# Layer 0 self attention of a two-layer block: norms of two groups' keys in three steps over three slots, and rounds of a choice spread over three slots

## The chip, the cores and the metric

The kernel runs on one core of one Trainium2 chip. The metric is device time in microseconds (us) of one execution, as the median of several. Five engines with instruction streams of their own matter: TensorE (PE; its weight loads are PEld), VectorE (DVE), ScalarE (ACT), GpSimd (POOL) and SyncE (SP), which here only issues DMAs. Each engine works its stream off in order, and waits on semaphores for the others.

## The reference, cut to what matters

The input is `x`, 64 sequences of 32 tokens of 256 features. Two layers follow, each a cross attention, a self attention and a feed-forward part, each added to `x`. The change lies in the stage of layer 0's self attention, during which the choice of blocks for layer 0's feed-forward part is made as well:

```python
x = x + _L0_attn_ref(_layernorm(x, axis=-1), g_norm, Wq, Wkv, Wout, g_out)
x = x + _L0_ffn_ref(_layernorm(x, axis=-1), Wr, br, W1, W2)

def _L0_attn_ref(x, g_norm, Wq, Wkv, Wout, g_out):   # 16 heads of 128, one k and v for all
    xn = _layernorm(x, g_norm)
    q = xn @ Wq
    k, v = split(xn @ Wkv)
    q = l2norm(q * 16) * 4
    k = l2norm(k) * 4
    attn = softmax(q k^T)                             # within one sequence of 32
    return _layernorm(merge_heads(attn @ v) @ Wout, g_out)

def _L0_ffn_ref(x, Wr, br, W1, W2):
    prob = softmax(x @ Wr.T + br)                     # 16 blocks of 64
    mask = ones at the 4 largest of prob, ties to the lower block
    h = gelu(x @ W1.T) * mask of the block
    return h @ W2.T
```

The self attention sees two layer norms in a row: the block's own, and the one inside with `g_norm`. Both need a reciprocal root of a variance plus 1e-5; the second variance follows from the first, as variance times the square of the first reciprocal root.

## The kernel before, in words

The 2048 tokens lie in 16 tiles `xs[0..15]` of 128 tokens by 256 features, in SBUF throughout; four tiles are a group (`g` 0 to 3). All arithmetic is float32.

The stage of layer 0's self attention ("stage B", tile pools `wB`, `psB`, `psBy`, `psB2`) has its order on TensorE, VectorE, ScalarE and GpSimd written out by hand: these four engines take their instructions in the order in which the Python code issues them (`tc.manual_schedule`). SP's order is made by a scheduler. The stage is a loop over slots `t` = 0 to 16. In the trace I let slot `t` begin with the first scores (`Sb`, L908) of tile `t`. A slot issues, in this order:

- `similar(t)`: scores `Sb` and sums of squares `ssb` (L916, from `q2b`, which GpSimd squared); then ScalarE's Sqrt of them (`rqb`, L925)
- `gather(t - 1)`: the weighted sums of the values for the tile before, `avb` (L955), with shares `pTb` that VectorE finished in the slot before (L945); VectorE and ScalarE copy them to `oTb`, two parts each (L960, L962)
- `scale(t)`: VectorE's reciprocal of `rqb` (L930, 3.34 us) and its product with the scores (L932)
- `square(t + 1)` on GpSimd (L896, four parts), then `power(t)`: ScalarE's Exp (L936)
- place 5, where extra steps are put
- `project(t - 1)`: 32 matmuls `yb` (L968), about 7.1 us; `norm_stats(t - 1)`: statistics of `yb` on VectorE and a Sqrt on ScalarE (`lns_bo`, L980)
- `share(t)`: sums of the exponentials (`denb`, L942), VectorE's reciprocal of them (L944, 3.35 us) and the product into `pTb` (L945)
- `norm_out(t - 1)`: VectorE makes `ynb` (L992); GpSimd multiplies it by the gain and adds it to `xs` (L993, L994)
- `rotate(t)`: nine products on GpSimd (L822 to L839) of some 10 us in all, for layer 1; `fetch(t + 1)`: DMA loads for the next; `write_pad(t)`: a DMA

Between them are the places 0 to 4. `query_part` at the places 0 to 3 makes the queries of later tiles (`qb`, L877; copied by ScalarE, L885), some ten parts ahead. Further steps go to a slot and a place with `at(slot, place, step)`; steps of one slot and place run in the order of their `at` calls. Two PSUM buffers with the tag `mm` are shared in turn by `qb`, `kvp`, `kTp`, the transposes `tp` and `tpr`, `hp`, `lpc` and `mTp`: a matmul into one waits until the buffer's last content was copied out.

The steps that bear on the change:

- `keys_norm(g)`, at (3, 5) for g = 2 and at (6, 5) for g = 3: statistics of four tiles on VectorE (`stats`, L174 and L175), both norms one after the other (`ln_group` with `twice=True`: `rstd_of` is an addition on VectorE, L163, a Sqrt on ScalarE, L165, and a reciprocal on VectorE, L167; two products, L183 and L184, between them), then ScalarE writes the four normed tiles (`ln_out`, L196). `keys_turn(g)` transposes them a slot or two later, at (4g - 4, 2), and `keys_of` makes keys and values (`kvp`, L364), `turn_keys` turns the keys.
- `choose_norm(g)`, at (4g + 5, 5): the norm for the choice, statistics and one Sqrt (`lnv_r`, `lns_r`, `lnr_r`, `lnh_r`), then four outputs of ScalarE (`xn_r`, L196). `choose_turn(g)`, at (4g + 6, 1): transposes (`tpr`, L642) and ScalarE's copies (`xTr`, L645).
- `choose_blocks(g)`, at (4g + 7, 5): matmuls `lpc`, a softmax of 16 values.
- `choose_best(g, work, rounds)`: each of four rounds (0 to 3) finds the largest value left and adds its block to the mask. A round is two reductions (L679, L684), three or more products and comparisons of 128 x 64 with two inputs (L681, L682, L688), for rounds 0 to 2 a SCALAR_TENSOR_TENSOR that takes the block out (L690), and for rounds 1 to 3 an addition to the mask (L692). For groups 0 and 1, rounds 0 and 1 are at (4g + 7, 5) and 2 and 3 at (4g + 8, 5). Group 2 has its first two at (15, 3).
- `choose_store(g)`, at (4g + 9, 2): four transposes of the mask (`mTp`, L699), VectorE's copy (L701), a DMA to `maskd` in DRAM (L702). `spread` reads it back, one row for 64 partitions, as `mb` (L708).
- From slot 13 on the feed-forward part of group 0 is worked in: `hp` (L716), ScalarE's Gelu (L723), VectorE's product with `mb` (L724).

Phase A, before this stage, has the other form of the reciprocal root, with `power=True`: an addition and a power of -0.5 on GpSimd (L159, L160).

Of the kernel before, what the change touches and what calls it, by code (L numbers as in the profile page):

```python
# [7 lines left out]
F32 = mybir.dt.float32  # L8
AF = mybir.ActivationFunctionType
ALU = mybir.AluOpType  # L10
# [3 lines left out]
P = 128  # L14
B, S, D = 64, 32, 256
NT = B * S // P
NG = NT // 4
# [10 lines left out]
EPS = 1e-5  # L28
# [11 lines left out]
def bc(ap, axis, n):  # L40

    shape = list(ap.shape)
    shape.insert(axis, n)
    return ap.unsqueeze(axis).to_broadcast(shape)
# [3 lines left out]
def perceiver_kernel(ctx: ExitStack, tc: tile.TileContext, a: dict, out: bass.AP):  # L48
    nc = tc.nc
# [21 lines left out]
    def sm(name, shape):  # L71
        return small.tile(shape, F32, tag=name.split("_")[0], name=name)
# [4 lines left out]
    xs = [x[:, :D] for x in xf]  # L77
# [69 lines left out]
    mhalf = const.tile([P, 4], F32, name="mhalf")  # L147
# [22 lines left out]
    def stats(mv_slot, src, name, sign=None):  # L170
        st = sm(f"lnb_{name}", [P, 6])
        if sign is not None:
            nc.vector.tensor_copy(st[:, 0:1], sign)
        nc.vector.bn_stats(st, src)  # L174
        nc.vector.bn_aggr(mv_slot, st)  # L175
# [16 lines left out]
    def ln_out(x_, rs, sh, i, name, act=False):  # L192

        y = xnp.tile([P, D], F32, tag="xn", name=f"xn_{name}_{i}")
        if act:
            nc.scalar.activation(  # L196
                y, x_, AF.Identity, scale=rs[:, i : i + 1], bias=sh[:, i : i + 1]
            )
        else:
            nc.vector.scalar_tensor_tensor(  # L200
                y,
                x_,
                rs[:, i : i + 1],
                sh[:, i : i + 1].to_broadcast([P, D]),
                ALU.mult,
                ALU.add,
            )
        return y

    def ln_group(g, name, twice=False, act=False, power=False, sign=None):  # L210

        mv = sm(f"lnm_{name}{g}", [P, 4, 2])
        for i in range(4):
            stats(mv[:, i, :], xs[4 * g + i], f"{name}{g}_{i}", sign)
        rs, sh = ln_scale(mv, f"{name}{g}", twice, power)
        return [ln_out(xs[4 * g + i], rs, sh, i, f"{name}{g}", act) for i in range(4)]
# [127 lines left out]
    latT = {}  # L344
# [4 lines left out]
    def keys_norm(g):  # L349
        latT[g] = ln_group(g, "b", twice=True, act=True, power=g == 0)  # L350

    def keys_turn(g, ps):
        latT[g] = transposed(latT[g], ps, g, "b", gain=gn)

    def keys_of(g, ps, part):

        xT = latT[g]
        if part == 0:
            keys[g] = kvp.tile([P, 4, D], F32, tag="kv", name=f"kvb{g}"), sm(f"ssk_b{g}", [P, 4])
        kv, ssk = keys[g]  # L360
        for i in range(2 * part, 2 * part + 2):
            kv_ps = ps.tile([P, D], F32, tag="mm", name=f"kvp{g}_{i}")
            for k in range(KC):
                nc.tensor.matmul(  # L364
                    kv_ps,
                    xT[:, k, i * P : (i + 1) * P],
                    b_kv[:, k, :],
                    start=(k == 0),
                    stop=(k == KC - 1),
                )  # L370
            nc.scalar.copy(kv[:, i, :], kv_ps)
            junk = kvp.tile([P, P], F32, tag="junk", name=f"junkb{g}_{i}")
            nc.scalar.activation(junk, kv[:, i, :P], AF.Square, accum_out=ssk[:, i : i + 1])
        if part == 1:
            sk = sm(f"sk_b{g}", [P, 4])
            nc.scalar.activation(sk, ssk, AF.Sqrt, bias=keps, scale=1.0 / 16.0)
            rk = sm(f"rk_b{g}", [P, 4])
            nc.vector.reciprocal(rk, sk)
            for i in range(4):
                nc.vector.tensor_scalar_mul(kv[:, i, :P], kv[:, i, :P], rk[:, i : i + 1])  # L380
            keys[g] = kv

    def turn_keys(g, ps):
        kv = keys[g]
        kT_ps = ps.tile([P, 512], F32, tag="mm", name=f"kTp{g}")
        for i in range(4):
            nc.tensor.transpose(kT_ps[:, i * P : (i + 1) * P], kv[:, i, :P], ident)
        kT = kvp.tile([P, 512], F32, tag="kT", name=f"kTb{g}")
        nc.vector.tensor_copy(kT, kT_ps)
        keys[g] = kT, kv  # L390
# [4 lines left out]
    with tc.tile_pool(name="wA", bufs=2) as work, tc.tile_pool(  # L395
        name="psA", bufs=1, space=PSUM
    ) as ps1, tc.tile_pool(
        name="psA2", bufs=2, space=PSUM
# [234 lines left out]
    def choose_norm(g, act=True):  # L633
        choice[g] = ln_group(g, "r", act=act)

    def choose_turn(g, ps, work):
        xn = choice[g]
        xT = choice[g] = work.tile([P, KC, 512], F32, tag="xTr", name=f"xTr{g}", bufs=1)
        for k in range(KC):
            tp = ps.tile([P, 512], F32, tag="mm", name=f"tpr{g}_{k}")  # L640
            for i in range(4):
                nc.tensor.transpose(  # L642
                    tp[:, i * P : (i + 1) * P], xn[i][:, k * P : (k + 1) * P], ident
                )
            nc.scalar.copy(xT[:, k, :], tp)  # L645
        return xT
# [28 lines left out]
    def choose_best(g, work, rounds):  # L675

        lg, mx, mask = choice[g]
        for r in rounds:
            nc.vector.tensor_reduce(mx, lg, AX.X, ALU.max)  # L679
            eq = work.tile([P, 4, 16], F32, tag="eq", name=f"eqc{g}_{r}", bufs=1)  # L680
            nc.vector.tensor_tensor(eq, lg, bc(mx, 2, 16), ALU.is_equal)  # L681
            nc.vector.tensor_tensor(eq, eq, bc(desc, 1, 4), ALU.mult)  # L682
            m2 = sm(f"m2c_{g}_{r}", [P, 4])
            nc.vector.tensor_reduce(m2, eq, AX.X, ALU.max)  # L684
            one = mask
            if r:
                one = work.tile([P, 4, 16], F32, tag="one", name=f"onec{g}_{r}", bufs=1)
            nc.vector.tensor_tensor(one, eq, bc(m2, 2, 16), ALU.is_equal)  # L688
            if r < 3:
                nc.vector.scalar_tensor_tensor(lg, one, -2.0, lg, ALU.mult, ALU.add)  # L690
            if r:
                nc.vector.tensor_add(mask, mask, one)  # L692

    def choose_store(g, ps, work):

        mask = choice.pop(g)[2]
        mT_ps = ps.tile([16, 512], F32, tag="mm", name=f"mTp{g}")
        for i in range(4):
            nc.tensor.transpose(mT_ps[:, i * P : (i + 1) * P], mask[:, i, :], ident)  # L699
        mT = const.tile([16, 512], F32, tag="mT", name=f"mTc{g}", bufs=1)  # L700
        nc.vector.tensor_copy(mT, mT_ps)  # L701
        nc.sync.dma_start(maskd[g], mT)  # L702
# [142 lines left out]
    with tc.tile_pool(name="wB", bufs=2) as work, tc.tile_pool(  # L845
        name="psB", bufs=1, space=PSUM
    ) as ps1, tc.tile_pool(name="psBy", bufs=1, space=PSUM) as ps_y, tc.tile_pool(
        name="psB2", bufs=2, space=PSUM
# [164 lines left out]

        steps = {}

        def at(slot, place, fn):
            steps.setdefault((slot, place), []).append(fn)

        for g in range(1, NG):
            at(4 * g - 4, 2, lambda g=g: keys_turn(g, ps2))
            slot, place_ = (0, 5) if g == 1 else (4 * g - 3, 1)
            at(slot, place_, lambda g=g: keys_of(g, ps2, 0))
            at(4 * g - 3, 3, lambda g=g: keys_of(g, ps2, 1))
            at(4 * g - 2, 2, lambda g=g: turn_keys(g, ps2))
            if g > 1:
                at((3, 6)[g - 2], 5, lambda g=g: keys_norm(g))
        for g in range(NG - 1):
            at(4 * g + 5, 5, lambda g=g: choose_norm(g))  # L1030
            at(4 * g + 6, 1, lambda g=g: choose_turn(g, ps2, work))
            at(4 * g + 7, 5, lambda g=g: choose_blocks(g, ps2, work))
            if g < NG - 2:
                at(4 * g + 7, 5, lambda g=g: choose_best(g, work, (0, 1)))
            at(4 * g + 8, 5, lambda g=g: choose_best(g, work, (2, 3)))
            if g < NG - 2:
                at(4 * g + 9, 2, lambda g=g: choose_store(g, ps2, work))
        ff, late = {}, []

        def ff_late():  # L1040
# [96 lines left out]
    with tc.tile_pool(name="wC", bufs=2) as work, tc.tile_pool(  # L1137
        name="psCh", bufs=2, space=PSUM
# [95 lines left out]
        latT = {}  # L1234
# [98 lines left out]
    with wd1:  # L1333
# [6 lines left out]
        with tc.tile_pool(name="wD", bufs=2) as work, tc.tile_pool(  # L1340
            name="psD", bufs=1, space=PSUM
        ) as ps1, tc.tile_pool(
            name="psD2", bufs=2, space=PSUM
# [288 lines left out]
            for pair in range(NB // 2):  # L1632


                b = 2 * pair
# [330 lines left out]
    with tc.tile_pool(name="wE", bufs=2) as work, tc.tile_pool(  # L1966
        name="psE", bufs=1, space=PSUM
# [7 lines left out]
        ps2 = ps1  # L1975
# [572 lines left out]
```

## Time and profile before

| what | value |
|---|---|
| three runs | 1151.64, 1155.46, 1159.72 us; median 1155.46 |
| profiled execution, its own time | 1160.48 us |
| its span, first to last instruction | 1158.6 us |
| mean granted TensorE clock | 0.984 |
| stage B in that span | about 145 to 486 us |

What the engines did in some slots (start of the slot to the next, in us; the shares of idle time follow by subtraction):

| slot | from, to | TensorE busy | VectorE busy | ScalarE busy | GpSimd busy |
|---|---|---|---|---|---|
| 1 | 159.33, 179.13 | 19.80 | 12.13 | 10.15 | 2.56 |
| 2 | 179.13, 197.56 | 18.43 | 10.91 | 7.99 | 14.87 |
| 3 | 197.56, 216.30 | 18.23 | 17.96 | 7.51 | 15.45 |
| 4 | 216.30, 237.86 | 19.16 | 14.10 | 10.81 | 14.68 |
| 6 | 259.89, 279.75 | 19.62 | 16.06 | 11.07 | 15.44 |
| 7 | 279.75, 299.53 | 19.78 | 17.74 | 7.81 | 15.42 |
| 8 | 299.53, 320.61 | 19.16 | 19.99 | 8.58 | 13.98 |
| 9 | 320.61, 343.31 | 22.25 | 19.54 | 12.79 | 16.89 |
| 11 | 363.18, 382.96 | 19.78 | 17.22 | 7.45 | 15.44 |
| 12 | 382.96, 403.61 | 19.15 | 19.84 | 8.48 | 14.32 |
| 13 | 403.61, 422.84 | 18.89 | 17.55 | 11.14 | 15.06 |
| 14 | 422.84, 443.60 | 19.26 | 15.85 | 13.60 | 18.21 |

How to read the lines of the profile: a line of the page's first part is an engine, its busy time, its share of the span and its number of instructions. A line of the table of waits is who waited for what: us in total, how often, the longest. A line of the timeline is start, duration, engine, line of the kernel, operation, output `<-` inputs, shapes and count; merged neighbours have one line, and in square brackets stands the idle time of the engine just before it and what ended that.

### The profile page before, as it was taken

Reading aid. Unit: us, or ns where it says so; the run is one execution under the profiler, and the core shown is the slowest. Engines: PE = TensorE matmul, PEld = TensorE weight load, DVE = VectorE, ACT = ScalarE, POOL = GpSimd, SP = SyncE. Lnnn points to the kernel's source line nnn. Section 1 sums busy time; section 2 is a strip of 40 time slices with the busy share of each in tenths; the row PEclk is TensorE's granted clock in tenths of the full one; section 3 lists DMA queues with packets and bytes.
Section 4 is the critical chain, followed back from the end, with each engine's and each line's share of the span. In section 5 each row is a group of like instructions: output and inputs, shape, how many; then the busy total and the mean of one; then the engine's idle time right before and its main releaser. Section 6 shows DMA issues by size and latency. Waiting matters only on the chain. (4 is left out here: it accounts for less than half of the span.)

```text
span 1158.6 us, 26394 instructions
## 1 busy us (share of the span) xinstructions
PE 1106.6 (96%) x10026; PEld 790.2 (68%) x10026; DVE 769.7 (66%) x1812; ACT 575.4 (50%) x1442; POOL 457.0 (39%) x766
## 2 busy tenths in 40 slices
PE   9999999899999999999998999999999989889997
PEld 5667766677767657667676777777777657555653
DVE  5786246868987987765215787777878565765532
ACT  2346363545355365231227777777777456542221
POOL 1444255777768787410001121121222356732111
PEclk9999999999999999999999999999999998989999
DMA  5131132546346446492213121223230044212413
GB/s 133 57 95 40 33 88 85 171 123 168 97 129 206 116 116 191 144 278 69 74 39 66 29 56 29 74 56 83 56 83 19 4 133 126 86 35 74 153 38 118
DMA packets 98990, 109.05 MB, mean 94 GB/s; under 512 B 37240, under 2 KB 73465, under 8 KB 98642
## 3 DMA queue, kind: packets, MB, share of 16 engines
q1 hardware_dynamic: 97138, 103.05, 31.5%
q0 software_dynamic: 1728, 4.33, 1.1%
q8 instruction: 80, 1.31, 0.5%
q14 instruction: 44, 0.36, 0.1%
HBM read 76.36 MB, written 31.41 MB: 93 GB/s over the span
## 5 line engine op out<-in xcount | busy, mean ns | idle before, releaser
L1469 ACT ACTIVATE pp<-Sd,nm 128x256 f32<-128x256 f32 x256 | 119.9, 482 | 40.4 <-POOL nm L1466 40.4
L877 PE MATMUL qb<-xT_b,b_q 128*128 128x256 f32 x512 | 122.2, 386 | 0.8 <-ACT qTb L885 0.8
L877 PEld LDWEIGHTS qb<-xT_b,b_q 128*128 128x128 f32 x512 | 94.9, 191 | 40.1 <-issue 19.3
L1465 DVE TENSOR_REDUCE nm<-Sd 128x2 f32<-128x512 f32 x128 | 79.5, 684 | 54.1 <-PE Sd L1452 54.1
L968 PE MATMUL yb<-b_o,oTb 128*128 128x256 f32 x512 | 114.9, 383 | 0.5 <-DVE oTb L960 0.5
L1466 POOL TENSOR_SCALAR nm<-nm 128x2 f32<-128x2 f32 x128 | 27.0, 211 | 221.6 <-DVE nm L1465 221.3
L968 PEld LDWEIGHTS yb<-b_o,oTb 128*128 128x128 f32 x512 | 97.2, 192 | 14.7 <-issue 1.6
L1487 DVE TENSOR_TENSOR pp<-pp,rd 128x512 f32<-128x512 f32 x128 | 89.6, 700 | 4.4
L1497 PE MATMUL pt<-cst,pp 128*128 128x128 f32 x512 | 68.3, 275 | 6.2 <-DVE pp L1487 5.2
L1503 ACT COPY pTd<-pt 128x512 f32<-128x512 f32 x128 | 68.8, 591 | 10.4 <-PE pt L1497 4.8
L896 POOL TENSOR_TENSOR q2b<-qTb 128x512 f32<-128x512 f32 x64 | 64.7, 1041 | 13.9 <-ACT qTb L885 13.9
L1497 PEld LDWEIGHTS pt<-cst,pp 128*128 128x128 f32 x512 | 59.4, 141 | 15.7 <-ACT ld L1477 5.0
L885 ACT COPY qTb<-qb 128x512 f32<-128x512 f32 x64 | 37.3, 584 | 63.9 <-PE qb L877 61.1
L930 DVE RECIPROCAL rqb<-rqb 128x512 f32<-128x512 f32 x16 | 53.5, 3344 | 17.1 <-ACT rqb L925 17.1
L1245 PE MATMUL qd<-xT_d,d_m 128*128 128x256 f32 x256 | 63.8, 393 | 0.7 <-DVE rd L1486 0.3
L1544 PE MATMUL yd<-d_n,co 128*128 128x256 f32 x256 | 63.2, 391 | 0.0
L1478 POOL TENSOR_TENSOR sd<-sd,ld 128x2 f32<-128x2 f32 x128 | 27.4, 214 | 86.0 <-ACT ld L1477 86.0
L1452 PE MATMUL Sd<-ct,qTd 64*128 64x256 f32 x480 | 60.0, 388 | 0.0
L731 PE MATMUL yc<-c,hc 128*128 128x256 f32 x256 | 58.5, 382 | 0.0
L1518 PE MATMUL od<-pTd,na 128*64 128x256 f32 x480 | 58.4, 385 | 0.0
L1544 PEld LDWEIGHTS yd<-d_n,co 128*128 128x128 f32 x256 | 46.2, 189 | 16.7 <-DVE nm L1465 7.7
L944 DVE RECIPROCAL rdb<-denb 128x512 f32<-128x512 f32 x16 | 53.7, 3354 | 5.8 <-PE denb L942 5.6
(429 smaller groups left out, 2416.8 us busy)
## 6 DMA issues: line engine op xcount, KB each, us to landing
srt<-pad SPq DMA_DIRECT2D x17, 1040.0 KB
mb<-maskd SPq DMA_DIRECT2D x64, 128.0 KB
ct<-ctd SPq DMA_DIRECT2D x30, 257.0 KB
rct<-in_ctxT_dram SPq DMA_DIRECT2D x32, 128.5 KB
rrt<-in_ctxT_dram SPq DMA_DIRECT2D x64, 64.2 KB
ctd<-rct SPq DMA_DIRECT2D x32, 128.5 KB
nad<-rna SPq DMA_DIRECT2D x16, 256.0 KB
fg<-in_f_wg_dram SPq DMA_DIRECT2D x16, 256.0 KB
```

Of the source, the lines that this page charges most:

```text
L731: nc.tensor.matmul(y_ps, hs[f][:, i * P : (i + 1) * P], c_2[:, f, :], start=(f == 0), stop=(f == 7),)
L877: nc.tensor.matmul(q_ps[:, hh, :], b_q[:, k, h * P : (h + 1) * P], xT[:, k, c0 : c0 + 256], start=(k == 0), stop=(k == KC - 1),)
L896: nc.gpsimd.tensor_tensor(q2[:, 4 * h4 : 4 * h4 + 4, :], q, q, ALU.mult)
L968: nc.tensor.matmul(y_ps, oT[:, h, :], b_o[:, h, :], start=(h == 0), stop=(h == NH - 1))
L1245: nc.tensor.matmul(q_ps[:, r, :], m[:, k, pr * P : (pr + 1) * P], xT[:, k, c0 : c0 + 256], start=(k == 0), stop=(k == KC - 1),)
L1452: nc.tensor.matmul(logits[b][hh][:, u, :], qT[hs, b % 8, 4 * u : 4 * u + 4, :], ct[hs, b % 4, :KEYS], start=True, stop=True,)
L1465: nc.vector.tensor_reduce(nm, s_ps[hh], AX.X, ALU.max, negate=True)
L1469: nc.scalar.activation(pb[:, u, hh, :], s_ps[hh][:, u, :], AF.Exp, bias=nm[:, u : u + 1], accum_out=sd[:, u : u + 1],)
L1487: nc.vector.tensor_tensor(pp, pp, bc(rd, 2, KEYS), ALU.mult)
L1497: nc.tensor.transpose(pts[c][:, hh * 256 + u * P : hh * 256 + u * P + P], probs[b][:, u, hh, c * P : (c + 1) * P], ident,)
L1503: nc.scalar.copy(pT[:, c, :], pt)
L1544: nc.tensor.matmul(y_ps, co[:, pr, :], n[:, pr, :], start=(pr == pr0), stop=(pr == pr0 + n_pr - 1),)
```

## The change

`keys_norm` of groups 2 and 3 is no longer one step of one slot. A new function `keys_norm_step(g, z)` has three: z = 0 takes the statistics and gives the first reciprocal root to GpSimd (an addition and a power); z = 1, a slot later, makes the second variance on VectorE and gives its reciprocal root to GpSimd; z = 2, another slot later, makes scale and shift on VectorE and has ScalarE write the tiles. The last step is in the slot and place in which all of it was before: slots 1, 2, 3 for group 2 and 4, 5, 6 for group 3. The small tiles between the steps are new ones of their own, four float32 values per partition each (eight for the statistics).

For groups 0 and 1 the four rounds are spread differently: round 0 stays in slot 4g + 7, rounds 1 and 2 are in slot 4g + 8, round 3 in slot 4g + 9, and `choose_store` is in slot 4g + 10 instead of 4g + 9, at place 2 as before. At (9, 5) and (13, 5) round 3 is issued ahead of `choose_norm` of the next group. Group 2 stays as it was.

```diff
+        begun = {}
+
+        def keys_norm_step(g, z):
+            if z == 0:
+                mv = work.tile([P, 4, 2], F32, name=f"kbm_{g}", bufs=1)
+                for i in range(4):
+                    stats(mv[:, i, :], xs[4 * g + i], f"b{g}_{i}")
+                r1 = work.tile([P, 4], F32, name=f"kbr_{g}", bufs=1)
+                nc.gpsimd.tensor_scalar(r1, mv[:, :, 1], EPS, None, ALU.add)
+                nc.gpsimd.tensor_tensor(r1, r1, mhalf[:, 0:4], ALU.pow)
+                begun[g] = mv, r1
+            elif z == 1:
+                mv, r1 = begun[g]
+                r2 = work.tile([P, 4], F32, name=f"kbq_{g}", bufs=1)
+                nc.vector.tensor_tensor(r2, mv[:, :, 1], r1, ALU.mult)
+                nc.vector.tensor_tensor(r2, r2, r1, ALU.mult)
+                nc.gpsimd.tensor_scalar(r2, r2, EPS, None, ALU.add)
+                nc.gpsimd.tensor_tensor(r2, r2, mhalf[:, 0:4], ALU.pow)
+                begun[g] = mv, r1, r2
+            else:
+                mv, r1, r2 = begun.pop(g)
+                nc.vector.tensor_tensor(r2, r2, r1, ALU.mult)
+                nc.vector.scalar_tensor_tensor(r1, mv[:, :, 0], -1.0, r2, ALU.mult, ALU.mult)
+                latT[g] = [ln_out(xs[4 * g + i], r2, r1, i, f"b{g}", True) for i in range(4)]
...
             if g > 1:
-                at((3, 6)[g - 2], 5, lambda g=g: keys_norm(g))
+                for z in range(3):
+                    at((1, 4)[g - 2] + z, 5, lambda g=g, z=z: keys_norm_step(g, z))
         for g in range(NG - 1):
             at(4 * g + 5, 5, lambda g=g: choose_norm(g))
             at(4 * g + 6, 1, lambda g=g: choose_turn(g, ps2, work))
             at(4 * g + 7, 5, lambda g=g: choose_blocks(g, ps2, work))
-            if g < NG - 2:
-                at(4 * g + 7, 5, lambda g=g: choose_best(g, work, (0, 1)))
-            at(4 * g + 8, 5, lambda g=g: choose_best(g, work, (2, 3)))
-            if g < NG - 2:
-                at(4 * g + 9, 2, lambda g=g: choose_store(g, ps2, work))
+            if g == NG - 2:
+                at(4 * g + 8, 5, lambda g=g: choose_best(g, work, (2, 3)))
+                continue
+            for z, rounds in enumerate(((0,), (1, 2), (3,))):
+                at(4 * g + 7 + z, 5, lambda g=g, rounds=rounds: choose_best(g, work, rounds))
+            at(4 * g + 10, 2, lambda g=g: choose_store(g, ps2, work))
```

## The prediction

> **What bounds the kernel now.** I read the busy shares first, then the waits of TensorE between 140 and 560 us, where the change lies, then each engine's timeline there, slot by slot.
>
> ```profile
> PE 1106.6 (96%) x10026; PEld 790.2 (68%) x10026; DVE 769.7 (66%) x1812; ACT 575.4 (50%) x1442; POOL 457.0 (39%) x766
> ```
>
> TensorE is the bound, so only idle time of TensorE can be won. Of the 420 us in that stretch, its waits for other engines add up to 11.5 us in the table of waits, and one row is nearly half of that (times, then the longest):
>
> ```profile
> PE avb L955 <- DVE pTb L945: 5.1, 3, 2.2
> ```
>
> The timeline shows the three places, the first matmuls of the weighted sums (`gather`) at the heads of slots 4, 8 and 12:
>
> ```profile
> 222.31 1.14 PE L955 MATMUL avb<-pTb,kvb 32*128 32x512 f32 x8 [2.16 <-DVE pTb L945]
> ...
> 305.06 1.14 PE L955 MATMUL avb<-pTb,kvb 32*128 32x512 f32 x8 [1.68 <-DVE pTb L945]
> ...
> 325.05 1.14 PE L955 MATMUL avb<-pTb,kvb 32*128 32x512 f32 x8
> ...
> 388.07 1.14 PE L955 MATMUL avb<-pTb,kvb 32*128 32x512 f32 x8 [1.26 <-DVE pTb L945]
> ```
>
> They are the slots after 3, 7 and 11: in 3 VectorE does `keys_norm(2)`, in 7 and 11 it does `choose_blocks` and two rounds. What else VectorE did there:
>
> ```profile
> 210.40 0.42 DVE L174 BATCH_NORM_STATS2 lnb_b<-x 128x6 f32<-128x256 f32 x1
> ...
> 212.65 1.03 DVE L163 TENSOR_SCALAR lnv_b<-lnm_b 128x4 f32<-128x4 f32 x1
> 213.96 0.18 DVE L167 RECIPROCAL lnr_b<-lns_b 128x4 f32<-128x4 f32 x1 [0.27 <-ACT lns_b L165]
> ...
> 217.44 0.43 DVE L174 BATCH_NORM_STATS2 lnb_bo<-yb 128x6 f32<-128x256 f32 x1
> ...
> 314.04 1.31 DVE L690 SCALAR_TENSOR_TENSOR lgc<-onec,lgc 128x64 f32<-128x64 f32 x1
> ...
> 324.27 0.69 DVE L945 TENSOR_TENSOR pTb<-pTb,rdb 128x512 f32<-128x512 f32 x1
> ```
>
> The norm of the keys occupies VectorE from 210.40 to 217.44, while the projection's result waited for it since 213.78 (the 7.14 us block of `yb` from 206.64). Slot 8 is the warning: VectorE ends its share at 324.96 and the sums start at 325.05 without a wait. It is as tight as a slot can be, and so is slot 12 (407.62 against 407.70).
>
> **Part 1: norms of the keys in three steps.** Slot 3 keeps two small operations (0.16 us each alone, up to 1 us beside GpSimd) of 7.04 us. The share then ends some 3.6 us earlier, bounded by the projection's end, and the 2.16 us go. GpSimd starts its next rotation as much earlier, so the squares for slot 5 are no longer late (from the scores at 237.86 to the sums of squares it is 1.28 us, elsewhere 0.88: 0.4 won). The moved pieces: four pairs of statistics, 2.1 us, go into slots 1 and 4, where VectorE sits idle 5.3 and 6.6 us for the projection; two products (0.16 to 0.96 us each) into slots 2 and 5, idle 5.1 and 2.4. These idle times are the cover; without it the 2.1 us would be late time of the share. The Sqrt of ScalarE becomes an addition and a power on GpSimd, 0.23 and 1.04 us by the rows of `lnr_b`. They queue ahead of `norm_out`'s two products, for which GpSimd idles anyway (14.3, 2.8, 2.1 and 5.9 us in slots 1, 2, 4, 5), and VectorE reads them a slot later. Slot 6 loses 6 us of VectorE but its sums had no wait. No table load goes: `lns_bo` needs the Sqrt table right after. Sum: -2.56 us (-2.0 to -2.6).
>
> **Part 2: rounds 0 | 1, 2 | 3.** Slots 7 and 11 lose round 1 (297.40 to 300.18, 2.78 us; 2.79 in slot 11), which covers the waits of 1.68 and 1.26. But slots 8 and 12 now hold rounds 1 and 2 for 2 and 3: one SCALAR_TENSOR_TENSOR more. It took between 0.22 and 1.31 us in this trace; I take 0.96, as the last operation of that place did (319.20). Slot 8: VectorE starts 1.15 us after the sums of the slot, then 18.56 us as before, plus 0.96: 20.67. TensorE alone needs 19.99 less the 0.64 by which late squares held it: 19.35. So 1.3 us of the wait come back: net 1.68 + 0.64 - 1.35 = 0.97 won (0.6 to 1.7). Slot 12 in the same way: 0.35 won (0 to 1.1).
>
> **Part 3: round 3 ahead of `choose_norm`, in slots 9 and 13.** A round of six operations took 1.5 us with GpSimd idle (467.25 to 468.79) and 4.7 or 4.8 beside its rotation. In slot 9 it starts at the phase at which round 2 started in slot 8; its first five operations took 2.45 us there, with the last 3.3. The store's copy and its wait (1.32) leave, so `choose_norm(1)` comes 2.0 us later (0 to 3.4). VectorE has room (1.46 us idle and 3.1 us ahead of the sums). Who waits is ScalarE, in order behind this norm's Sqrt and four outputs:
>
> ```profile
> 341.61 0.59 ACT L885 COPY qTb<-qb 128x512 f32<-128x512 f32 x1 [1.51 <-PE qb L877]
> ```
>
> This copy has 1.51 us of room; it slips to about 341.9, while TensorE, 0.6 us earlier without the transposes of the mask, asks for that PSUM buffer in `keys_of`: 0.6 us lost (0 to 2.0). Slot 13 is worse, since ScalarE is full there:
>
> ```profile
> 419.25 0.20 ACT L165 ACTIVATE lns_r<-lnv_r 128x4 f32<-128x4 f32 x1 [0.61 <-DVE lnv_r L163]
> 420.59 2.08 ACT L196 ACTIVATE xn_r<-x,lnh_r,lnr_r 128x256 f32<-128x256 f32 x4 [1.13 <-DVE lnh_r L189]
> 422.57 0.19 ACT L980 ACTIVATE lns_bo<-lnv_bo 128x1 f32<-128x1 f32 x1
> ...
> 424.07 0.60 ACT L723 ACTIVATE hc<-hp 128x512 f32<-128x512 f32 x1
> ...
> 427.98 0.60 ACT L723 ACTIVATE hc<-hp 128x512 f32<-128x512 f32 x1
> ...
> 429.83 1.09 ACT L645 COPY xTr<-tpr 128x512 f32<-128x512 f32 x2
> ```
>
> From 420.59 to 430.92 it idles only 0.29 us (ahead of its copy of the sums at 428.87), and `hp` at 430.48 waits 0.71 us for one of these copies. What delays `lnv_r` reaches TensorE whole. The masked product now ends at 415.7 instead of 416.7 (no copy of the mask, an earlier Gelu); a round beside GpSimd, 4.0 us taken between 1.5 and 4.8, makes the statistics 3.1 us late (0.5 to 3.9). Less the 0.29, `hp` slips 2.8 us.
>
> **Part 4: the store a slot later.** Four transposes (0.44 us net) and a copy of 0.68 us go from slots 9 and 13 to 10 and 14; VectorE idles 2.5 and 2.9 us there. In 10 the transposes follow two users of the two PSUM buffers and wait some 0.3 us for a copy. In 14 they stand between two `hp`, so the second waits for the first one's Gelu: 0.85 us with the transposes (0.4 to 1.0). On SP's queue the store moves from 345 to about 367, and ten of the mask's 16 reads (6.2 us to issue) with it, ahead of the rotation's write, which goes out at 372.8 as soon as GpSimd is done, and of the next fetch. Held up by at most 6 us, that fetch still lands some 15 us before its use after 408, and the masks, read at 415, are there by 380: taken at nothing. Without that room each late microsecond would be GpSimd's or the product's. The second store moves alike, for masks read after 486.
>
> Sum: -2.56 - 0.97 - 0.35 + 0.6 + 0.3 + 2.8 + 0.85 = **+0.7 us**. The profiled execution took 1160.48 us at a span of 1158.6, so 1161.2 against itself; it stands 5.0 above the median of 1155.46, from which the forecast is **1156.2 us**. After 560 us nothing is touched and the whole shifts.
>
> The round's price deserves a second look. In the trace the two-input operation at L682 took between 0.217 and 1.314 us, so even the worst did not wait much longer than one GpSimd operation of 1.28. The Trainium skill's page "SBUF — State Buffer" (section "SBUF: two separate sides") says that GpSimd and a VectorE operation with two SBUF inputs take the shared port pair by an exclusive lock and that the loser blocks for the whole instruction. An estimate by that rule: each of a round's four two-input operations could wait 1.28 us, 6.4 us in all, and the total would be +6 us. No round in this trace reached that; 4.8 us is the most.
>
> **Rivals.** *Rounds are cheap in their new places* (25%): one operation more costs 0.22, and round 3 costs 1.5 us. Then part 2 wins 1.7 and 1.1, slot 9 loses none, slots 13 and 14 lose 0.3 + 0.85: -2.56 - 1.7 - 1.1 + 0.3 + 1.15 = -3.9, 1151.6 us. For it: the round at 467. Against it: GpSimd rotates from 327 and from 410 on, through both places. *Slower by ScalarE's queue in slot 13* (20%): round 3 at 4.8 us and a contended `lnv_r` (1.0 for 0.34 us) make the Gelus and copies of slot 13 another 1.5 us late, and the copy of slot 9 costs 2.0 for 0.6: +3.6, 1159.1 us. It decides from 3.3 us for that round on, where the sum passes zero. For it: two-input operations of 1.0 to 1.3 us all through the rotation; against it: the 2.45 us of the five operations from 311.59. *GpSimd becomes late by the powers* (5%): four times 1.27 us ahead of a rotation, passed on to the squares, make +5.1 on top of the sum, 1161.3 us; for it the three late squares in the waits (1.5 us), against it the idle times above. The forecast has the remaining 50%. That the edits change nothing in the order can be excluded, since these engines run in written order.
>
> **Numbers.** The cases span -3.9 to +5.8; the three runs before spread 4 us to either side of their median, so a median of three may be 1.5 off. Eight in ten: 1150.5 to 1162. One per cent is 11.6 us, about what can be told from no change, and no case reaches it: within 95%, faster 2%, slower 3%, for what the trace of before cannot show, such as other addresses in SBUF.
>
> **What would show it.** Right: no wait of `avb` at the heads of slots 4, 8 and 12, a wait of about 1 us at 9 and at 13; `hp` of slot 14 waiting some 3 us for ScalarE. Wrong: `lnv_r` in slot 13 no later than 419 after the same start (then the faster rival), or waits on `q2b` in slots 2 to 5 (then GpSimd).

## The result, and the profile after

| | before | after |
|---|---|---|
| median | 1157.30 us (18 runs, 1151.64 to 1159.72) | 1161.89 us (18 runs, 1155.08 to 1167.35) |
| ratio to before | | 1.0035, 95% interval 1.0018 to 1.0052 |
| profiled execution, its own time | 1160.48 us | 1155.37 us |
| its span | 1158.6 us | 1153.6 us |
| mean granted TensorE clock in it | 0.984 | 0.989 |

So the change makes the kernel some 4 us slower, well within one per cent, while the one profiled execution of after is 5.1 us faster than that of before. The clock explains that pair. TensorE's granted clock is 1.0 or 0.5, and falls to 0.5 for steps of 3.41 us. The profiled execution of before has 36.1 us of such time within its span, that of after 25.8; half of the difference is 5.1 us. With time at half clock counted by half, the two are equal within 0.2 us. Below, "at full clock" means counted so, and "half-clock time" is twice (1 - mean clock) times the span. Over all runs it was 36.0 us after the change; before, it was 26 to 29 us on average, by the group of runs.

The stage itself is read from the first projection of tile 0 (L968) to that of tile 15, since all ahead of it varies by some microseconds from one execution to the next. At full clock that is 310.2 us before and 311.5 after: 1.3 us more. (Up to the first weighted sums of slot 15, before either profile has a halved step, it is 0.96 us.) The page's first part, then the waits of TensorE between 140 and 560 us, after:

```profile
PE 1103.2 (96%) x10026; PEld 787.4 (68%) x10026; DVE 761.7 (66%) x1804; ACT 574.6 (50%) x1438; POOL 461.6 (40%) x774
```

```profile
PE yb L968 <- DVE oTb L960: 3.5, 2, 3.0
PE ssb L916 <- POOL q2b L896: 1.9, 1, 1.9
PE avb L955 <- DVE pTb L945: 1.1, 1, 1.1
```

The 5.1 us of `avb` are down to 1.1. In their place stands a projection that waits for VectorE's copies `oTb`, 3.0 us at once. Before, that row read:

```profile
PE yb L968 <- DVE oTb L960: 0.5, 1, 0.5
```

The timeline of TensorE after, at the heads of slots 4, 8, 9, 12 and 13 and at that projection:

```profile
216.38 1.14 PE L955 MATMUL avb<-pTb,kvb 32*128 32x512 f32 x8
...
296.96 1.14 PE L955 MATMUL avb<-pTb,kvb 32*128 32x512 f32 x8
...
317.43 1.14 PE L955 MATMUL avb<-pTb,kvb 32*128 32x512 f32 x8 [1.07 <-DVE pTb L945]
...
379.52 1.14 PE L955 MATMUL avb<-pTb,kvb 32*128 32x512 f32 x8
...
388.60 7.17 PE L968 MATMUL yb<-b_o,oTb 128*128 128x256 f32 x32 [2.96 <-DVE oTb L960]
...
402.14 1.14 PE L955 MATMUL avb<-pTb,kvb 32*128 32x512 f32 x8
```

The waits at 4, 8 and 12 are gone, and 1.07 us has come back at 9, as forecast; at 13 nothing came back. What held the copies, on VectorE in slot 12:

```profile
378.38 0.54 DVE L992 TENSOR_SCALAR ynb<-yb,lnm_bo,lnr_bo 128x256 f32<-128x256 f32 x1
386.95 0.28 DVE L137 MEMSET pad<- 128x260 f32 x1 [8.02 <-DMA srt<-pad]
387.26 0.69 DVE L960 COPY oTb<-avb 128x512 f32<-128x512 f32 x1
```

`write_pad` fills one constant tile anew for every token tile and writes it to DRAM (1040 KB). The MEMSET may not touch the tile before the last write has read it, and it stood idle 8.02 us for that. In the profile of before the same MEMSET has no wait:

```profile
388.74 0.28 DVE L137 MEMSET pad<- 128x260 f32 x1
```

The cause is on SP, whose queue works in order. Before:

```profile
345.44 0.37 SPq L702 DMA_DIRECT2D maskd<-mTc  x1
348.04 6.21 SPq L708 DMA_DIRECT2D mb<-maskd  x10
354.35 0.53 SPq L140 DMA_DIRECT2D srt<-pad  x1
...
366.75 4.13 SPq L708 DMA_DIRECT2D mb<-maskd  x6
370.98 0.54 SPq L140 DMA_DIRECT2D srt<-pad  x1
```

And after:

```profile
357.85 0.37 SPq L702 DMA_DIRECT2D maskd<-mTc  x1
361.13 6.22 SPq L708 DMA_DIRECT2D mb<-maskd  x10
...
377.31 3.82 SPq L708 DMA_DIRECT2D mb<-maskd  x6
381.23 0.54 SPq L140 DMA_DIRECT2D srt<-pad  x1
```

The store of the mask and its 16 reads stand one tile further down, so the write of the pad goes out at 381.23 for 370.98, although the kernel runs 7.2 us ahead there (3.7 of it from before the stage, 3.5 won in it). Relative to the work around it, it is over 17 us late.

### The profile page after: what moved, and what is told of

It is laid out like the page before. It is cut to its first block, busy times and chain, and to the rows that moved or that the text cites. A ratio compares the mean times of both kernels' runs of the same rounds, so it can differ in the third digit from the quotient of the medians.

```text
span 1153.6 us, 26392 instructions
## 1 busy us (share of the span) xinstructions
PE 1103.2 (96%) x10026; PEld 787.4 (68%) x10026; DVE 761.7 (66%) x1804; ACT 574.6 (50%) x1438; POOL 461.6 (40%) x774
## 5 line engine op out<-in xcount | busy, mean ns | idle before, releaser
L968 PE MATMUL yb<-b_o,oTb 128*128 128x256 f32 x512 | 115.5, 384 | 3.6 <-DVE oTb L960 3.5
L968 PEld LDWEIGHTS yb<-b_o,oTb 128*128 128x128 f32 x512 | 97.5, 192 | 18.5 <-DVE oTb L960 3.2
```

What stands on the lines that cost most here:

```text
L968: nc.tensor.matmul(y_ps, oT[:, h, :], b_o[:, h, :], start=(h == 0), stop=(h == NH - 1))
```

## The experiments

All in one table: the stage at full clock is read from the profile of each, the half-clock time is the mean over its runs, and the ratio is to runs of before beside it on the same chip.

| kernel | runs | median us | ratio to before | stage at full clock | half-clock us |
|---|---|---|---|---|---|
| before (run again) | 12 | 1158.82 | 1.0000 [0.9986, 1.0014] | 310.2 | 28.2 |
| after | 18 | 1161.89 | 1.0035 [1.0018, 1.0052] | 311.5 | 36.0 |
| after (run again) | 12 | 1160.58 | 1.0024 [1.0005, 1.0044] | 311.1 | 33.1 |
| norms_only | 6 | 1149.99 | 0.9937 [0.9913, 0.9961] | 307.2 | 18.4 |
| rounds_only | 12 | 1166.70 | 1.0061 [1.0043, 1.0080] | 314.0 | 34.5 |
| store_late | 7 | 1163.10 | 1.0067 [1.0043, 1.0091] | 313.7 | 32.5 |
| two_pads | 9 | 1164.10 | 1.0061 [1.0037, 1.0084] | 307.7 | 34.3 |
| pad_once | 12 | 1153.81 | 0.9978 [0.9959, 0.9997] | 308.9 | 27.8 |
| rounds_g0 | 12 | 1155.83 | 0.9993 [0.9975, 1.0012] | 309.2 | 26.2 |
| rounds_g1 | 12 | 1155.23 | 0.9988 [0.9969, 1.0007] | 309.8 | 26.3 |
| round3_behind | 12 | 1159.73 | 1.0034 [1.0014, 1.0053] | 312.2 | 28.0 |
| kept_busy | 12 | 1161.21 | 1.0035 [1.0018, 1.0053] | 313.2 | 28.6 |
| blocks_early | 12 | 1156.59 | 1.0000 [0.9978, 1.0022] | 310.2 | 23.9 |

### The two parts alone, and both kernels again

norms_only is the changed kernel with the rounds and the store as before; rounds_only is the kernel before with the new rounds and store.

```diff
 norms_only against after
-            if g == NG - 2:
-                at(4 * g + 8, 5, lambda g=g: choose_best(g, work, (2, 3)))
-                continue
-            for z, rounds in enumerate(((0,), (1, 2), (3,))):
-                at(4 * g + 7 + z, 5, lambda g=g, rounds=rounds: choose_best(g, work, rounds))
-            at(4 * g + 10, 2, lambda g=g: choose_store(g, ps2, work))
+            if g < NG - 2:
+                at(4 * g + 7, 5, lambda g=g: choose_best(g, work, (0, 1)))
+            at(4 * g + 8, 5, lambda g=g: choose_best(g, work, (2, 3)))
+            if g < NG - 2:
+                at(4 * g + 9, 2, lambda g=g: choose_store(g, ps2, work))
 rounds_only against after
-                for z in range(3):
-                    at((1, 4)[g - 2] + z, 5, lambda g=g, z=z: keys_norm_step(g, z))
+                at((3, 6)[g - 2], 5, lambda g=g: keys_norm(g))
```

> The kernel before, unchanged, for a second profile and for the granted clock of each execution. Theory A (the stalls of stage B alone make the difference): its executions have the same mean clock as those of the changed kernel (0.9845) and lie 1 to 2 us below them at the same clock. Theory B (the clock makes most of it): its mean clock is higher, about 0.987, as each step of the clock costs some 1.85 us and 4.6 us between the medians would be two to three steps. In its stage B no VectorE wait for the DMA of the pad tile.

> The changed kernel, unchanged, for a second profile. Theory C (SP's queue): the wait of VectorE's memset for the pad's DMA at the end of slot 11 (8.0 us in the first profile, 3 us of it TensorE's) is there again, between 5 and 10 us. If it was an accident of one execution: below 1 us. Ratio to before 1.002 to 1.005.

> The norms in three steps alone, rounds and store as before. Prediction's part 1: the wait at the head of slot 4 (2.16 us) and the 0.4 us of late squares for slot 5 go, the waits of 1.7 and 1.3 us at the heads of slots 8 and 12 stay: 2.6 us faster, ratio 0.9977. If the clock falls wherever TensorE is kept busier (theory B): less than 1.5 us faster, at a lower mean clock than before.

> The rounds over three slots and the store a slot later alone, norms of the keys in one step. Theory C: slots 7 to 14 lose what they lost in the changed kernel, so 3.6 us slower, ratio 1.003, with VectorE's wait for the pad's DMA at the end of slot 11. Prediction's parts 2 to 4 (ScalarE's queue in slot 13 instead, no wait on a DMA): 3.3 us slower, with the loss in slots 13 and 14 and a gain of 0.35 us over slots 11 and 12.

In the stage the parts add up: 3.0 us less and 3.8 us more make 0.8, for the 0.9 to 1.3 of the whole. In time they do not: 0.63% less and 0.61% more would make nothing, and the whole is 0.24 to 0.35% slower. The norms alone beat both kernels (0.9937, at least 4 us by the interval). Of their 7 us, 3.0 are in the stage; the rest comes with 10 us less half-clock time, which none of the expectations had. In the one profile of norms_only the steps that are missing against before stand mostly outside of the stage, at code that the edit does not touch; why is not known. So theory B, that the clock falls where TensorE is kept busier, does not hold for this run (mean clock 0.992). Between before and after the clock does differ: the mean clock of before, run again, is 0.9878, that of after, run again, 0.9858. (A halved step costs 1.7 us, not 1.85.) The MEMSET waits 8.49 us in the changed kernel run again and 8.20 in rounds_only, and not at all in norms_only, where TensorE's waits read:

```profile
PE avb L955 <- DVE pTb L945: 2.6, 2, 1.4
PE tp_c L244 <- DVE x L738: 1.0, 1, 1.0
PE ssb L916 <- POOL q2b L896: 0.8, 1, 0.8
```

The two waits left are those of slots 8 and 12, 1.35 and 1.25 us: what the rounds were to take away.

### Who makes the pad late

store_late is the kernel before with nothing but the store a slot later:

```diff
-                at(4 * g + 9, 2, lambda g=g: choose_store(g, ps2, work))
+                at(4 * g + 10, 2, lambda g=g: choose_store(g, ps2, work))
```

> The kernel before with only the store of the mask a slot later, rounds and norms as before. Theory C: the wait for the pad's DMA is there, 5 to 9 us, and 3 us of it TensorE's: work 3.5 us above before (with the 0.3 and 0.85 us of the transposes' new places), and more time at half clock: ratio 1.003 to 1.006. Prediction's part 4: 1.15 us, no wait for a DMA.

One number is changed, and the stage grows by 3.5 us; spreading the rounds as well (rounds_only) adds 0.3. The ratio, 1.0067, lies a little above the 1.003 to 1.006 that were expected. On VectorE in slots 12 and 13 of store_late:

```profile
396.30 0.28 DVE L137 MEMSET pad<- 128x260 f32 x1 [6.11 <-DMA srt<-pad]
...
414.27 0.28 DVE L137 MEMSET pad<- 128x260 f32 x1 [1.06 <-DMA srt<-pad]
```

So the store alone carries the wait. The rounds are not needed for it.

two_pads gives the pad tile two buffers of the stage's pool, so that the MEMSET waits for the write before last:

```diff
-    pad = const.tile([P, DP], F32, name="pad")
...
-    def write_pad(n_):
+    def write_pad(n_, pool):
+        pad = pool.tile([P, DP], F32, tag="pad", name=f"pad{n_}", bufs=2)
...
-            write_pad(t)
+            write_pad(t, work)
```

> The changed kernel with two pad tiles in turn (from the stage's own pool) in place of one, so that VectorE's memset waits for the write of two slots ago. Theory C (the reads of the mask, now ahead of the pad's write on SP's queue, hold VectorE through that tile): the wait of 8 us at the end of slot 11 goes, the projection of slot 12 starts without its 3 us, and as the rounds of slot 12 then stand beside GpSimd again, some 1 us of wait comes back: work (span less half of the time at half clock) 2 us below the changed kernel's 1142.5. Theory B (the stall in slot 12 is what the clock falls after): time at half clock falls from 35 us to 29 or below, so the ratio to before is 0.999. Theory A' (ScalarE's queue alone): nothing changes, 1.003.

In the stage this did what it should: 307.7 us for 311.5, no wait of the projection, and 1.43 us back at the head of slot 13. The time rose all the same, by a wait that the edit itself brought. The stage's pool is released at its end, and ScalarE's next step has to wait for the last write of the pad (timeline of ScalarE):

```profile
486.38 0.20 ACT L978 ACTIVATE lns_bo<-lnv_bo 128x1 f32<-128x1 f32 x1 [9.41 <-DVE lnv_bo L976]
493.14 1.28 ACT L721 ACT_TABLE_LOAD   x1 [6.56 <-DMA srt<-pad]
```

`hp` waits 6.54 us for that, at 495.09, and two halved steps begin during that wait, at 492.65. The half-clock time stayed at 34.3 us, where theory B expected 29 or less, so this run does not decide on the clock. The tile's content never changes, so pad_once fills it once instead:

```diff
-        nc.vector.memset(pad, 0.0)
-        nc.vector.memset(pad[:, D : D + 1], 2.0 * B * S)
+        if n_ == 0:
+            nc.vector.memset(pad, 0.0)
+            nc.vector.memset(pad[:, D : D + 1], 2.0 * B * S)
```

> The changed kernel, with the two MEMSETs of the pad tile written once, ahead of tile 0, instead of for every tile: the same data goes out, but VectorE never again waits for SP's queue. Theory (the store a slot later puts SP's queue late, and VectorE waits at that MEMSET): the wait of 8.0 to 8.5 us at the end of slot 11 is gone, the projection of slot 11 waits for no oTb, and slot 12 starts its sums 3.0 us earlier against the changed kernel; about 1.1 us come back at the head of slot 13, since rounds 1 and 2 then run beside GpSimd (4.2 us and more each pair instead of 1.5 each). Nothing waits at the end of the stage, unlike with two pad tiles. Span less half of the half-clock time: 1 to 2 us under the changed kernel's 1141.6 to 1143.3; ratio to before 0.998 to 1.001. Rival (the wait only stood in front of something that was late anyway): slot 12 still loses 2 to 3 us, ratio 1.002 to 1.005 as the changed kernel's.

Slot 12 and the head of slot 13 on TensorE, in pad_once:

```profile
381.34 1.14 PE L956 MATMUL avb<-pTb,kvb 32*128 32x512 f32 x8
...
387.30 7.07 PE L969 MATMUL yb<-b_o,oTb 128*128 128x256 f32 x32
...
401.81 1.14 PE L956 MATMUL avb<-pTb,kvb 32*128 32x512 f32 x8 [1.07 <-DVE pTb L946]
```

The projection waits for nothing, and the forecast's 1.1 us stands at the head of slot 13. The stage is 2.3 to 2.6 us shorter than the changed kernel's, a little more than expected, the half-clock time is back to that of before, and the ratio is at the lower end of what was expected. The mean span less half of the half-clock time, 1138.2 us, is 3.4 to 5.1 us under the changed kernel's, where 1 to 2 were expected; the same figure varies by 1.8 us between groups of runs of before. The rival falls: the wait at the pad was the loss itself.

rounds_g0 and rounds_g1 leave the new rounds and the late store to one group:

```diff
+            if g != 0:                      # rounds_g1: g != 1
+                at(4 * g + 7, 5, lambda g=g: choose_best(g, work, (0, 1)))
+                at(4 * g + 8, 5, lambda g=g: choose_best(g, work, (2, 3)))
+                at(4 * g + 9, 2, lambda g=g: choose_store(g, ps2, work))
+                continue
```

> The changed kernel with the new rounds and the late store for group 0 alone (slots 7 to 10); group 1's rounds and store stand as before (slots 11 to 13). Theory: the MEMSET of the pad waits about 8 us at the end of slot 11 as in the changed kernel, because it is group 0's store that puts SP's queue late, and slot 12 loses about 3 us; slots 13 and 14 lose nothing (3.8 us in the changed kernel). The stage ends 1 to 4 us under the changed kernel's +0.9. Rival (the wait at the pad comes of the rounds of slot 11): no wait at the MEMSET.

> The changed kernel with the new rounds and the late store for group 1 alone (slots 11 to 14); group 0's stand as before (slots 7 to 9). Theory: no wait at the pad's MEMSET at the end of slot 11 and no loss of 3 us in slot 12; the wait of 1.3 us at the head of slot 12 is gone and some 1 us comes back at the head of slot 13; slots 13 and 14 lose the 3 to 4 us that they lose in the changed kernel, by the round in front of the norms and the transposes of the mask between two hp. The stage ends within 1 us of before (norms -3.3, slots 7 to 9 unchanged, then +3 to +4). Rival (slots 13 and 14 are late because slot 12 was): they lose under 1.5 us and the stage ends 2 to 4 us earlier than before.

VectorE's MEMSET in slot 12, first in rounds_g0, then in rounds_g1:

```profile
390.91 0.28 DVE L137 MEMSET pad<- 128x260 f32 x1 [5.58 <-DMA srt<-pad]
```

```profile
382.97 0.28 DVE L137 MEMSET pad<- 128x260 f32 x1
```

It is group 0's store that holds the pad, as expected, with a wait of 5.58 us for 8: VectorE, which here has two rounds in slot 11 as before, comes to the MEMSET 2.6 us later, while the write lands at the same time within the stage. TensorE waits behind it in rounds_g0:

```profile
392.56 8.75 PE L968 MATMUL yb<-b_o,oTb 128*128 128x256 f32 x32 [1.78 <-DVE oTb L960]
```

Slot 12 then loses 3.4 us: 1.78 of stall, and a step at half clock from 392.4 that costs 1.7. In rounds_g1 that loss is absent, 1.42 us come back at the head of slot 13, and slots 13 and 14 still lose 2.8 (3 to 4 expected). So their loss does not come from a late slot 12, and that rival falls. In rounds_g0 the first weighted sums of slot 15 come at +0.4 us against before, which looks like a miss (one to four under +0.96 were expected); at full clock, without that halved step, it is -1.3, as expected.

### Slots 13 and 14

round3_behind puts round 3 behind `choose_norm` in the same place:

```diff
-            for z, rounds in enumerate(((0,), (1, 2), (3,))):
+            for z, rounds in enumerate(((0,), (1, 2))):
...
+        for g in range(NG - 2):
+            at(4 * g + 9, 5, lambda g=g: choose_best(g, work, (3,)))
```

> The changed kernel with round 3 issued behind choose_norm in slots 9 and 13 instead of ahead of it. Prediction's part 3 (ScalarE's queue): the waits of TensorE that hang on it in slots 13 and 14 go (0.8 for xTr, 0.2 for a Gelu, and the second half of the weighted sums at 422 which took 2.35 for 1.14 us): 2.2 us faster than the changed kernel in work. If those come from GpSimd and VectorE being late there (theory C), less than 0.5 us.

The win did not come. From the projection of slot 13 to that of slot 14 it loses 3.8 us like the changed kernel (the transposes of the mask, now in slot 14, are counted in it). `choose_norm` is early, but now the round stands ahead of the next step in that place, `norm_stats`, and ScalarE's `lns_bo` waits for it with the same table loads queued behind it:

```profile
416.44 2.08 ACT L196 ACTIVATE xn_r<-x,lnh_r,lnr_r 128x256 f32<-128x256 f32 x4 [1.13 <-DVE lnh_r L189]
421.37 0.20 ACT L980 ACTIVATE lns_bo<-lnv_bo 128x1 f32<-128x1 f32 x1 [2.85 <-DVE lnv_bo L978]
421.59 1.28 ACT L723 ACT_TABLE_LOAD   x1
```

So it is not the order of the two steps, and by the expectation's own measure, less than 0.5 us won, the loss does not hang on `choose_norm` being late. In both places tried, the four microseconds of VectorE ahead of the statistics in slot 13 reach ScalarE, and through it TensorE.

### The clock

kept_busy puts 12 spare matmuls, which nothing reads, into the 3-us stall:

```diff
+        def busy(n_):
+            spare = ps2.tile([P, 256], F32, tag="mm", name="spare")
+            for _ in range(n_):
+                nc.tensor.matmul(spare, ident, cst[:, 0:256], start=True, stop=True)
+
+        at(12, 5, lambda: busy(12))
```

> The changed kernel with 12 spare matmuls (128 x 256, about 2.9 us; they add work that the reference has not, and nothing reads them) in TensorE's stall of 3 us ahead of the projection of slot 11. Clock theory (the clock is halved for 3.4 us after a stretch of the fixed grid with more than 1.7 us of idle TensorE): the stage's other waits and the span less half of the half-clock time stay as the changed kernel's (1141.6 to 1143.3, within 1 us), but no half-clock step between 386 and 400 us, and 2 to 4 us less half-clock time on average than the changed kernel's 33 to 36: 1 to 2 us faster than it although it does more, ratio to before 1.001 to 1.003. Rival (the halved steps come of something else): half-clock time as the changed kernel's, and a time that is the same or up to 1 us longer.

TensorE at the place of the stall, in kept_busy:

```profile
387.89 5.44 PE L1068 MATMUL spare<-cst 128*128 128x256 f32 x24
393.17 7.07 PE L968 MATMUL yb<-b_o,oTb 128*128 128x256 f32 x32
```

I had sized it wrongly: the 12 matmuls stand as 24 in the trace and took 5.44 us, not 2.9. The copies were ready at 391.24, so the projection began 1.9 us later than it could, and the stage grew by 1.7 to 2.1. For this the time did not rise: half-clock time fell from 33 to 36 us to 28.6, and the profile has no halved step between 386 and 400. (The first profile of after had none there either; the second had one, at 386.42.) That speaks for the clock theory, whose number for half-clock time (2 to 4 less) was too small; that the kernel becomes faster was a miss. As more than the stall was filled, it is no clean proof.

### A try to better the change

blocks_early keeps the norms, moves `choose_blocks` a slot up for groups 0 and 1 (slots 6 and 10), and leaves the rounds and the store as before:

```diff
-            at(4 * g + 7, 5, lambda g=g: choose_blocks(g, ps2, work))
+            at(4 * g + (6 if g < NG - 2 else 7), 5, lambda g=g: choose_blocks(g, ps2, work))
```

> The norms in three steps, rounds and store as before, and choose_blocks of groups 0 and 1 a slot earlier (slots 6 and 10, place 5), where the norms left VectorE idle 6 us or it idles 2.5. Stalls of VectorE's share as bound: slots 7 and 11 lose 2.5 us of VectorE, the waits of 1.7 and 1.3 us at the heads of slots 8 and 12 go: work 2.5 us below norms alone (1139.5), ratio to before 0.991. If the work is only moved into slots 8 and 12, as tight as before: the ratio of norms alone, 0.9937.

It gives back what the norms win in the stage. The two waits of `avb` that were to go are longer, on TensorE's timeline at the heads of slots 8 and 12:

```profile
302.18 1.14 PE L955 MATMUL avb<-pTb,kvb 32*128 32x512 f32 x8 [2.03 <-DVE pTb L945]
...
386.36 1.14 PE L955 MATMUL avb<-pTb,kvb 32*128 32x512 f32 x8 [2.04 <-DVE pTb L945]
```

Two things eat what was to be won. Round 1 stands beside GpSimd's squares for its whole length (293.06 to 297.09 on GpSimd) and took 4.2 us, where it had taken 2.8 before, its last operations behind them; round 0 took 4.9, for 4.8. And the 16 matmuls `lpc` of `choose_blocks` left slot 7 as well: TensorE's own work there is shorter by some 1.8 us, so it is ready for the shares sooner. VectorE wins 2.5 less 1.4 us there, TensorE 1.8, and the wait at slot 8 is 0.7 us longer than in norms_only. The best kernel remains norms_only.

## Why the prediction was right, and where it was not

It said no difference that can be told, 0.7 us more; measured are 0.35% [0.18, 0.52] more, 4 us. The median of 1161.89 is 0.1 us inside the range of 1150.5 to 1162, and that took luck: the sum lacks two costs, a wait and the clock (the last two points), and the range was wide enough for them because of other rivals and of the spread between runs. The stage came out at 0.96 for 0.67 because errors cancelled: one term was 2.0 us too low, the others together 1.7 too high. The shift against before, read at the first weighted sums of slots 6, 11, 13 and 15, in us (pad_once's last row less the 1.7 us of one halved step in slot 14):

| slots | forecast | after | pad_once | rounds_g1 |
|---|---|---|---|---|
| 3 to 5 (norms) | -2.56 | -2.65 | -3.06 | -2.65 |
| 7 to 10 | -0.07 | -0.87 | -0.87 | -0.74 (norms alone -0.68) |
| 11, 12 | -0.35 | **+1.66** | -0.50 | -0.15 |
| 13, 14 | +3.65 | +2.82 | +2.7 | +2.82 |
| sum | +0.67 | +0.96 | -1.7 | -0.72 |

- *Norms.* Right, in the waits named and in size (2.65 for 2.56). The cover named for the moved pieces held: no `q2b` wait in slots 2 to 5, so the rival "GpSimd late by the powers" is out.
- *Rounds.* Right in the waits: those at slots 8 and 12 went, and the one operation more brought 1.07 us back at the head of slot 9 (forecast 1.35) and, where the pad is out of the way, 1.07 at the head of 13 (forecast about 1). But the sum books 0.64 us under the rounds, for late squares, that the norms alone bring: in norms_only that wait is gone too, and 0.68 us are won in slots 7 to 10. The rounds and the store win another 0.2 there.
- *Slot 9.* The 0.6 us did not come. This is the copy of the prediction, in the same place of its slot:

```profile
331.14 2.08 ACT L196 ACTIVATE xn_r<-x,lnh_r,lnr_r 128x256 f32<-128x256 f32 x4 [0.91 <-DVE lnh_r L189]
...
333.55 0.59 ACT L885 COPY qTb<-qb 128x512 f32<-128x512 f32 x1 [0.24 <-PE qb L877]
```

Its room of 1.51 us has shrunk to 0.24: ScalarE was late by some 1.3, and the room just covered it. It starts 21.0 us behind the slot's first scores in both kernels. The step that it "slips to about 341.9" made too much of the round.

- *Slots 13 and 14.* The mechanism was right, the size 0.8 too large. Round 3 took 4.1 us (409.74 to 413.86) for 4.0, and ScalarE's Sqrt of `lnv_r` starts 18.0 us after the slot does, for 15.6 before: 2.4 later, where I had 3.1. The transposes between two `hp` cost 0.85 as put (428.61 to 429.46). What looks different is the wait. I had announced one of 3 us at `hp`; it is spread over several places of TensorE's timeline:

```profile
419.29 1.07 PE L916 MATMUL ssb<-q2b,ones 128*32 128x512 f32 x8 [1.89 <-POOL q2b L896]
...
422.20 2.35 PE L955 MATMUL avb<-pTb,kvb 32*128 32x512 f32 x8
...
425.34 0.66 PE L642 MATMUL tpr<-cst,xn_r 128*128 128x128 f32 x4 [0.20 <-ACT hc L723]
426.79 1.98 PE L716 MATMUL hp<-xT_c,c 128*128 128x512 f32 x4 [0.80 <-ACT xTr L645]
428.61 0.60 PE L699 MATMUL mTp<-cst,maskc 128*16 128x128 f32 x4
429.46 1.98 PE L716 MATMUL hp<-xT_c,c 128*128 128x512 f32 x4 [0.25 <-ACT hc L723]
```

GpSimd's squares are 1.1 us later than in norms_only (1.89 for 0.80); the sums take 2.35 us for 1.14, since their last two wait for ScalarE's `rqb`; the rest is ScalarE's. The late squares are no loss of their own: ScalarE works without a gap from 417.30 to 427.2, and in round3_behind, with squares 0.8 us less late, the loss is the same. Had I looked for the one wait alone, I would have taken the loss for absent. The rival with 3.6 us in all, from a dearer round 3, did not come about: that round took 4.1 us here and 3.6 in slot 9, where the copy cost nothing; in the kernel run again it did take 4.8 in slot 13, and the stage was no longer for it (311.1 us for 311.5).

- *The store on SP.* Here the prediction failed. It moved the store and the reads down the queue, counted their 6.2 us, and took them "at nothing", because the fetch and the masks had room; "without that room each late microsecond would be GpSimd's or the product's". The queue held one transfer that the list left out, the write of the pad, and the one who waits for its landing was VectorE, through a MEMSET of its source. That is 2.0 us in slots 11 and 12 (1.66 for -0.35), or 2.3 to 2.6 of the stage against pad_once (0.4 of it in slots 3 to 5, where pad_once only saves VectorE the MEMSETs); store_late shows that the store alone causes it.
- *The clock.* The sum had no term for it. Half of the half-clock time beyond that of before, 2 to 5 us over the runs, is most of the 4 us between the medians. The mean spans less that half are 1141.6 and 1143.3 us after, 1141.2 to 1143.0 before: at full clock the two kernels cannot be told apart by their times, and the stage's 1 us is seen in the profiles alone. The 3-us stall explains a part: one halved step costs 1.7. In the kernel run again it is seen (last section), and pad_once, which has no such stall, is back at 27.8 us. But round3_behind has a stall of 3.2 us at the same place and only 28.0 us of half-clock time, and norms_only has 18.4 with the same later stages. How the rest of the steps come to fall where they do is not settled.

## What to carry to other kernels

A DMA that moves down an in-order queue makes late every transfer behind it, and each has two users: who reads what it brings, and who wants to overwrite what it was reading. List both for each, one-buffer constants that are refilled included. Try the parts of a change alone before taking the sum: here one part wins 0.63%, and the two together lose 0.24 to 0.35%. And split the time of a run into work and half-clock time before comparing two profiles, or one profile tells the wrong sign.

## What the hardware showed

A stall of TensorE can cost more than its length. The clock is granted in a fixed grid of 3.41 us. Two executions of the changed kernel have the same stall, by the view of busy time in windows laid on that grid (from:to, length, then busy time of PE, PEld, DVE, ACT, POOL, granted clock, DMA share, GB/s). In the profiled run of after it falls across two windows, of which TensorE is idle 1.62 and 1.58 us:

```profile
383.61:387.02 3.41, 1.79 (x12) 1.19 (x10) 0.07 (x1) 2.40 (x4) 3.25 (x5) 1.00 0.89 266
387.02:390.44 3.42, 1.84 (x9) 1.63 (x10) 3.38 (x5) 0.54 (x1) 3.26 (x3) 1.00 0.30 69
390.44:393.85 3.41, 3.41 (x17) 3.02 (x16) 3.31 (x5) 1.26 (x2) 3.41 (x5) 1.00 0.49 142
```

In the run again it lies in one, idle 2.86 us, and the next is granted half the clock:

```profile
382.99:386.40 3.41, 0.55 (x4) 0.30 (x4) 1.04 (x4) 2.19 (x3) 3.25 (x5) 1.00 0.78 206
386.40:389.82 3.42, 2.85 (x7) 2.32 (x8) 3.42 (x2) 0.00 (x0) 3.34 (x5) 0.50 0.10 37
```

Over the 14 profiles of this case, laid on the grid, all 37 windows at full clock with over 1.9 us of idle TensorE (the last of each profile left out) were followed by a halved one, and of the 4507 followed by a full one none had over 1.9. Between 1.7 and 1.9 both occur. Another 44 halved steps follow windows with less than 1.7 us by the records, mostly in other stages, so this is not the whole rule.

The Trainium skill's page "TensorE: Matmul & The Clock Gate" (section "Part 1: The HAM clock gate (the "warmup" mystery)") has the free-running window of 3413 ns, which the grid here agrees with, and lets the clock fall after one idle window of about 3.4 us. The rows above differ: a little over half a window of idle time was enough, in rounds_g0 by a stall of 1.78 us.
